# Queries two chunks ahead, weights, gates and o placed behind the turning of a chunk, and z added in the third group of weights

## The chip, the cores and the metric

The kernel is one program on one core of a Trainium2 chip. The metric is the device time of one execution in microseconds (us): the median of three runs before was 2944.49 us (2940.36 to 2946.38). The core has the engines TensorE (PE; its weight loads are listed apart as PEld), VectorE (DVE), ScalarE (ACT) and GpSimd (POOL), and SyncE (SP), which here only issues DMAs. Each engine works through its own instructions in their order and waits on semaphores for the others. A DMA is issued by an engine (here SP and POOL) and moved by 16 DMA engines.

## The reference

With N = 1250 nodes, D = 1024 features, E = 40000 edges, the program computes a graph convolution and then one transformer layer with experts:

```
x = x + gnn(layernorm(x))            # h = x W^T + b, normalised sum over the edges and self loops
z = layernorm(x)
q, k = rope(z Wq[h]), rope(z Wk[h])  # 16 heads of 64
gv = top2of8(sigmoid(z Wsel_v[h]))   # a gate for each of 8 experts, all but two are 0
v = sum_e gv[e] * (z Wv[h, e])
o = softmax(q k^T / 8) v
go = top2of8(sigmoid(z Wsel_o[h]))
src = z + sum_h sum_e go[h, e] * (o Wo[h, e])
src = ln(src, ln1); out = x + ln(src + relu(src W1 + b1) W2 + b2, ln2)
```

All is in float32. The kernel gets this accuracy from matmuls of a rounded part ("hi") and a remainder ("lo") of each operand: a product is three matmuls (`dot`, L152 to L156), and every operand passes through a copy to hi on ScalarE and a subtraction to lo on VectorE.

## The kernel before

Three stages matter here. All of them lie in blocks of `manual_schedule`, in which every engine, and SP's and POOL's queues of DMAs with them, keeps exactly the order in which the Python code creates the instructions. The code is written as generators that are advanced piece by piece, so a place in a generator is a place in every queue.

**`values` (L872) beside `attention` (L711).** `values` makes v for one head after the other: 40 pieces a head, each of six 512-column matmuls. The expert weights of the next head come as four blocks of 512 KB: `load` (SP, into one of the two `w_raw` buffers), then `first_part` (the copy to hi, ScalarE, L138), then `second_part` (the subtraction to lo, VectorE, L144). The lists of pairs say at which of the 40 pieces each happens for each of the four blocks. Because there are two buffers, a load waits until the `second_part` of the block before the last is done.

`attention` works in 80 chunks (16 heads by 5 chunks of 256 queries), in eight pieces a chunk, and one piece of it is advanced after each piece of `values`. It starts at piece 26, so chunk n's piece p (0 to 7) stands behind `values` piece k where (k - 26) mod 8 = p. The pieces of a chunk n, with what they do for the chunks n - 1 and n - 2 that are still on their way:

- 0: `softmax(n, 0)`: scores of 128 queries (PE, L739), their maximum (DVE, L742), the exponential (ACT, L743); then `load_queries(n + 1)` (POOL)
- 1: `product(n - 2, 2)` (PE, L796); `turn_blocks(n - 1)`: two transposes on DVE (L816)
- 2: `product(n - 2, 3)`; `split(n - 1, 0)` and `(n - 1, 1)`: hi on ACT (L773)
- 3: `softmax(n, 1)`; `load_keys` where the next chunk opens a head; `rest(n - 1, 0)` and `(n - 1, 1)`: lo on DVE (L778)
- 4: `product(n - 2, 4)`, which ends with a copy of o on ACT (L803) and one or two DMAs of o to HBM (POOL); `turn(n)`; after the last chunk of a head the sums (SP); `split(n - 1, 2)`
- 5 to 7: the rest of the splits, and `product(n - 1, 0)` and `(n - 1, 1)`

`turn(n)` (L746) moves the exponentials p into the buffer `turned` by 16 DMAs of 80 KB, each of which brings a block of 32 partitions to another 32: eight on SP and eight on POOL. Then the transposes turn the blocks of 32 by 32 inside. `product(n - 1, 0)` writes to the PSUM tile `po`, of which there is one: it has to wait until the copy of o of the chunk before has read it.

**`outputs` (L935).** 16 groups of weights (8 pairs of heads, two halves of the experts), each with five steps of 250 nodes: 80 steps. A step has two tiles of 125 nodes by two halves of 512 columns: four results of 12 matmuls, each of which is added to the accumulator of its tile (`acc`, L1036). A step takes a block of the next group's weights (SP, 512 KB; not in the fifth step), `gb`, the gates of the step after the next (SP, two DMAs, 500 KB), and the attention's o with its sums for that step (SP, four DMAs or more, `load_o`). `gated` multiplies gates and o (DVE, L967 to L969), and `parts_of` makes hi and lo of it (L976, L978). Each step is eight pieces. The accumulators start as z: `acc_load` reads a tile of z from HBM by two DMAs (`move`, L150), and in the first group it stands two tiles ahead of the tile's first addition. The memory of the accumulators is that of zT, which `values` has read to its end by then.

The first sixteen pieces of `outputs` only prepare; they are advanced with the last 16 of `values`. Then the remaining 42 pieces of `attention` alternate with the first 42 of `outputs`: the first group, and a little. From then on `outputs` runs alone.

**`feed_forward` (L1049)**, after the last group. Its tables (`ftab`) are broadcast rows of 512 KB, loaded by SP.

`tc.issue_after(ins)`, which the change uses, adds an order (no semaphore, no wait for an end) between `ins` and those instructions created in its block that run on the engine of `ins`.

Of the kernel before, what the change touches and what calls it, by code (L numbers as in the profile page):

```python
# [2 lines left out]

# [8 lines left out]
F32 = mybir.dt.float32  # L12
# [5 lines left out]
ALU = mybir.AluOpType  # L18
# [54 lines left out]
def gnn_ffn_kernel(  # L73
# [631 lines left out]


    v_of = {}

    def attention(pool):

# [102 lines left out]

        def turn_blocks(n):
            for i in range(2):
                nc.vector.transpose(turned[n][:, i], turned[n][:, i])  # L816

        load_keys(0)
        load_queries(0)
        for n in range(len(chunks) + 2):  # L820
            now, last, before = (0 <= m < len(chunks) for m in (n, n - 1, n - 2))

            if now:
                softmax(n, 0)
            if before:
                rest(n - 2, 4)
            if n + 1 < len(chunks):
                load_queries(n + 1)
            yield
            if before:  # L830
                product(n - 2, 2)
            if last:
                turn_blocks(n - 1)
            yield
            if before:
                product(n - 2, 3)
            if last:
                split(n - 1, 0)
                split(n - 1, 1)
            yield  # L840
            if now:
                softmax(n, 1)
                if n + 1 < len(chunks) and chunks[n + 1][1] == 0:
                    load_keys(chunks[n + 1][0])
            if last:
                rest(n - 1, 0)
                rest(n - 1, 1)
            yield
            if before:
                product(n - 2, 4)  # L850
            if now:
                turn(n)
# [12 lines left out]
            if last:  # L865
                product(n - 1, 1)
                split(n - 1, 4)
                rest(n - 1, 3)
            yield


    def values(att_pool, pool, now):  # L872
# [8 lines left out]
        for h in range(H):  # L881
            raw, new = {}, [None] * 4

            def load(h, k, raw=raw):
                raw[k] = loaded(wv[h, k])

            def first_part(k, raw=raw, new=new):
                new[k] = high(raw[k])
# [3 lines left out]

            if h + 1 < H:

                for at_, k in ((22, 0), (36, 1), (37, 2), (39, 3)):
                    later(piece + at_, first_part, k)
                for at_, k in ((23, 0), (37, 1), (38, 2), (40, 3)):
                    later(piece + at_, second_part, k)
                for at_, k in ((16, 0), (22, 1), (28, 2), (37, 3)):
                    later(piece + at_, load, h + 1, k)  # L900
            v_of[h] = att_pool.tile([P, NT, P], F32R, name="v2", bufs=2)

# [29 lines left out]

    acc = []

    def outputs(acc_pool, pool):  # L935

        last = QW * (NC - 1)

# [43 lines left out]
        blocks = {k: [wo[j, 4 * half_e + i] for i in range(4)] for k, (j, half_e) in enumerate(order)}  # L982
        steps = [(k, c) for k in range(len(order)) for c in range(NQ)]

        def acc_load(t):
            acc.append(acc_pool(t))
            move(acc[t], z_d[t])

        def fetch(m, gates):
            if m < len(steps):  # L990
# [4 lines left out]
                    held[:] = load_o(j, c)  # L995


        w, raw, found, held, parts = [], [], [], [], []
        for begun in range(16):
            if begun < 2:  # L1000
                raw.append(loaded(blocks[0][begun]))
            if begun in (3, 4, 7, 8):
                w.append(rounded(raw.pop(0)))
            if begun in (3, 4):
                raw.append(loaded(blocks[0][begun - 1]))
            if begun == 4:
                fetch(0, True)
                fetch(0, False)
            if begun == 5:
                acc_load(0)  # L1010
            if begun == 9:
                current = gated(found.pop(0), *held)
                fetch(1, True)
                fetch(1, False)
            if begun in (11, 13):
                parts.append(parts_of(current, len(parts)))
            if begun == 14:
                acc_load(1)
            yield
        after = []  # L1020
        for m, (k, c) in enumerate(steps):
            raw = loaded(blocks[k + 1][c]) if c < 4 and k + 1 < len(order) else None
            following = m + 1 < len(steps)
            fetch(m + 2, True)
            for i in range(2):
                t = 2 * c + i
                if k == 0 and t + 2 < NT:
                    acc_load(t + 2)
                for half in range(2):
                    cols = slice(512 * half, 512 * half + 512)  # L1030
                    p = bank([KT, 512])
                    for e in range(4):
                        dot(p, [part[:, e, :] for part in parts[i]], [part[:, cols] for part in w[e]], e == 0, e == 3)
                        if e == 1:
                            yield
                    nc.vector.tensor_tensor(acc[t][:, cols], acc[t][:, cols], p, ALU.add)  # L1036
                    if following and half:
                        parts[i] = parts_of(current, i)
                    elif following and i == 0:
                        current = gated(found.pop(0), *held)  # L1040
                        fetch(m + 2, False)
                    elif raw is not None:
# [62 lines left out]

    f_ctx = ctx.enter_context(ExitStack())
    per_head = 4 * NT
    main, spare = [], []

    def acc_tile(t):  # L1110

# [10 lines left out]
    with tc.tile_pool(name="attp", bufs=1) as apool:  # L1122
        w = [weights(wv[0, k]) for k in range(4)]
        with tc.manual_schedule(engines=all_engines):
            heads = attention(apool)
            with tc.tile_pool(name="vpool", bufs=2) as vpool:
                for k, _ in enumerate(values(apool, vpool, w)):
                    if k >= per_head - lead:
                        next(heads)
                    if k == H * per_head - 4 * NZ - 1:  # L1130
                        z2_ctx.close()
                        ring[:0] = [ctx.enter_context(tc.tile_pool(name="ring2", bufs=3, side="right"))] * 3
                        gop = ctx.enter_context(tc.tile_pool(name="gop", bufs=1, side="right"))
                        main.append(outputs(acc_tile, gop))
                    elif main:
                        next(main[0])
            made = sum(1 for _ in zip(heads, main[0]))
    main = main[0]
    p_ctx.close()
    banks[:] = [5, 2]  # L1140
    psums.append(p_ctx.enter_context(tc.tile_pool(name="psum3", bufs=1, space=PSUM)))
    ftab = f_ctx.enter_context(tc.tile_pool(name="ftab", bufs=1))
    work = f_ctx.enter_context(tc.tile_pool(name="fwork", bufs=2))
    tail = feed_forward(ftab, work)
    with tc.manual_schedule(engines=all_engines):
        for _ in range(4 * (NT * (2 * NP - 1) + 4) - made):
            next(main)
    next(tail)
    for _ in main:
# [77 lines left out]
```

## Time and profile before

| | |
|---|---|
| median of three runs | 2944.49 us (2940.36 to 2946.38) |
| the profiled execution | 2949.87 us, its span 2948.1 us |
| granted clock of TensorE | 0.990 of full speed over the span |
| `values` beside `attention` | about 640 to 1840 us |
| first group of `outputs` beside the last chunks | about 1840 to 1970 us |
| `outputs` alone | about 1970 to 2780 us |
| VectorE's idle time before the transposes (L816) | 135.3 us |

The page of a profile lists for each engine its busy time. A group of instructions is given as line, engine, operation, output<-inputs, shape and count; then busy time, the mean of one in nanoseconds, the idle time of the engine just before them, and what ended most of it. A row of waits reads: who waited <- for whom: us in total, times, longest. A row of windows reads: stretch, its length, then the busy time and the number of instructions of PE, PEld, DVE, ACT and POOL, the granted clock of TensorE, the DMA engines' busy share, and GB/s. A row of the timeline reads: start, length, engine (SPq is SP's queue of DMA issues), line, operation, tiles, shape, count, and in brackets the idle time before it and what ended that. Rows of DMA queues give packets, MB and the share of the 16 engines' time.

### The profile page before, as it was taken

Reading aid. Unit: us, or ns where it says so; the run is one execution under the profiler, and the core shown is the slowest. Engines: PE = TensorE matmul, PEld = TensorE weight load, DVE = VectorE, ACT = ScalarE, POOL = GpSimd, SP = SyncE. Lnnn points to the kernel's source line nnn. Section 1 sums busy time; section 2 is a strip of 40 time slices with the busy share of each in tenths; the row PEclk is TensorE's granted clock in tenths of the full one; section 3 lists DMA queues with packets and bytes.
Section 4 is the critical chain, followed back from the end, with each engine's and each line's share of the span. In section 5 each row is a group of like instructions: output and inputs, shape, how many; then the busy total and the mean of one; then the engine's idle time right before and its main releaser. Section 6 shows DMA issues by size and latency. Waiting matters only on the chain. (4 is left out here: it accounts for less than half of the span.)

```text
span 2948.1 us, 40387 instructions
## 1 busy us (share of the span) xinstructions
PE 2845.5 (97%) x14018; PEld 2346.9 (80%) x14018; DVE 2118.5 (72%) x3588; ACT 996.7 (34%) x1708; POOL 570.3 (19%) x945
## 2 busy tenths in 40 slices
PE   6989999999999999999999999899999999999998
PEld 5777899978888887788888888677777777777787
DVE  7975786558777877878777777866566666666885
ACT  5772333324443433434343434421111111111222
POOL 2000011123333333333333333210000000000113
PEclk9999999999999999999999999999999999999999
DMA  3115466635645555555555555874444444444412
GB/s 118 57 44 159 146 182 177 191 90 137 154 130 147 133 136 123 128 149 138 146 138 139 139 145 126 213 204 126 115 120 122 115 119 122 112 122 117 112 53 88
DMA packets 229319, 385.45 MB, mean 131 GB/s; under 512 B 43369, under 2 KB 176489, under 8 KB 228946
## 3 DMA queue, kind: packets, MB, share of 16 engines
q1 hardware_dynamic: 176898, 273.49, 33.3%
q0 software_dynamic: 51888, 104.18, 14.6%
q10 hardware_dynamic: 320, 5.12, 0.6%
q8 instruction: 111, 1.82, 0.3%
q14 instruction: 102, 0.84, 0.1%
HBM read 220.73 MB, written 62.16 MB: 96 GB/s over the span
## 5 line engine op out<-in xcount | busy, mean ns | idle before, releaser
L155 PE MATMUL mm<-w_lo,zT 128*128 128x512 f32 (+2 forms) x1360 | 528.9, 389 | 3.8 <-DVE w_lo L144 3.3
L154 PE MATMUL mm<-w_hi,zT 128*128 128x512 f32 (+2 forms) x1360 | 529.7, 390 | 0.8 <-ACT w_hi L138 0.8
L156 PE MATMUL mm<-w_hi,zT 128*128 128x512 f32 (+2 forms) x1360 | 528.4, 389 | 0.0
L154 PE MATMUL mm<-w_hi,go_hi 128*125 128x512 f32 x1280 | 507.2, 396 | 3.7 <-ACT go_hi L976 2.8
L155 PE MATMUL mm<-w_lo,go_hi 128*125 128x512 f32 x1280 | 507.4, 396 | 0.0
L156 PE MATMUL mm<-w_hi,go_lo 128*125 128x512 f32 x1280 | 503.8, 395 | 0.0
L773 ACT CAST att_hi<-turned 128x512 fp32r<-128x512 f32 x400 | 239.9, 622 | 460.1 <-DVE turned L816 286.7
L754 POOL DMA_DIRECT2D turned<-p x640 | 343.9, 545 | 78.9 <-ACT p L743 44.5
L1036 DVE TENSOR_TENSOR zT<-zT,mm 125x512 f32<-125x512 f32 x256 | 175.5, 686 | 221.1 <-PE mm L156 216.8
L816 DVE STREAM_TRANSPOSE turned<-turned 128x1280 f32<-128x1280 f32 x160 | 232.4, 1491 | 135.3 <-DMA q<-kq_d 62.4
L976 ACT CAST go_hi<-gb 128x500 fp32r<-128x500 f32 x160 | 98.3, 616 | 660.0 <-PE mm L155 281.8
L742 DVE TENSOR_REDUCE most<-side 128x1 f32<-128x1250 f32 x160 | 231.0, 1444 | 111.7 <-PE side L739 109.1
L743 ACT ACTIVATE p<-side,most 128x1250 f32<-128x1250 f32 x160 | 209.2, 1308 | 290.3 <-DVE most L742 285.7
L156 PEld LDWEIGHTS mm<-w_hi,zT 128*128 128x128 f32 (+1 forms) x1360 | 253.1, 186 | 59.9
L154 PEld LDWEIGHTS mm<-w_hi,go_hi 128*125 128x125 f32 x1280 | 237.9, 186 | 65.2 <-ACT go_hi L976 3.5
L155 PEld LDWEIGHTS mm<-w_lo,zT 128*128 128x128 f32 (+1 forms) x1360 | 253.3, 186 | 43.9 <-DVE w_lo L144 8.6
L156 PEld LDWEIGHTS mm<-w_hi,go_lo 128*125 128x125 f32 x1280 | 237.9, 186 | 61.7 <-DVE go_lo L978 0.5
L155 PEld LDWEIGHTS mm<-w_lo,go_hi 128*125 128x125 f32 x1280 | 237.6, 186 | 58.2
L154 PEld LDWEIGHTS mm<-w_hi,zT 128*128 128x128 f32 (+1 forms) x1360 | 253.7, 187 | 35.6 <-ACT w_hi L138 1.0
L778 DVE TENSOR_TENSOR att_lo<-turned,att_hi 128x512 fp32r<-128x512 f32 x400 | 262.3, 681 | 0.0
L796 PE MATMUL po<-att_hi,v 128*128 128x256 f32 (+1 forms) x800 | 216.1, 291 | 38.1 <-ACT o L803 38.0
L144 DVE TENSOR_TENSOR w_lo<-w_raw,w_hi 128x1024 fp32r<-128x1024 f32 x154 | 189.4, 1231 | 35.7 <-ACT w_hi L138 35.2
(227 smaller groups left out, 4501.9 us busy)
## 6 DMA issues: line engine op xcount, KB each, us to landing
turned<-p SPq DMA_DIRECT2D x640, 80.0 KB
turned<-p POOLq DMA_DIRECT2D x640, 80.0 KB, 3.3
gb<-g_d SPq DMA_DIRECT2D x160, 250.0 KB
w_raw<-in_wv SPq DMA_DIRECT2D x64, 512.0 KB
w_raw<-in_wo SPq DMA_DIRECT2D x64, 512.0 KB
q<-kq_d POOLq DMA_DIRECT2D x80, 256.0 KB, 4.2
oc<-o_d SPq DMA_DIRECT2D x160, 125.0 KB
kq_d<-qk_hi SPq DMA_DIRECT2D x64, 156.2 KB
```

Source lines behind the costliest of these rows:

```text
L144: (lo_engine or nc.vector).tensor_tensor(lo, raw, hi.bitcast(F32), ALU.subtract)
L154: nc.tensor.matmul(p, lhsT=lhs[0], rhs=rhs[0], start=start, stop=False)
L155: nc.tensor.matmul(p, lhsT=lhs[0], rhs=rhs[1], start=False, stop=False)
L156: nc.tensor.matmul(p, lhsT=lhs[1], rhs=rhs[0], start=False, stop=stop)
L742: nc.vector.tensor_reduce(most, side[:, :N], AX.X, ALU.max, negate=True)
L743: nc.scalar.activation(p[:, (2 * n + i) % 3, :N], side[:, :N], AF.Exp, bias=most, accum_out=inverse[h][:, 2 * c + i : 2 * c + i + 1])
L754: queue.dma_start(t[NB * a : NB * (a + 1), :, KA * b : KA * (b + 1)], both[NB * b : NB * (b + 1), :, KA * a : KA * (a + 1)])
L773: nc.scalar.copy(hi, x)
L778: nc.vector.tensor_tensor(lo, x, hi.bitcast(F32), ALU.subtract)
L796: nc.tensor.matmul(po, lhsT=v_of[h][:rows, t, :], rhs=part[:rows, :, NB * b : NB * (b + 1)], start=(first and b == 0 and part is parts[0]) ...
L816: nc.vector.transpose(turned[n][:, i], turned[n][:, i])
L1036: nc.vector.tensor_tensor(acc[t][:, cols], acc[t][:, cols], p, ALU.add)
```

## The change

- `attention`: `load_queries` of the first two chunks at the start; that of chunk n + 2 in piece 3 of chunk n, after `softmax(n, 1)`, instead of that of n + 1 in piece 0.
- `turn_blocks` keeps its last transpose in `landed`. The loads of `values`, and in `outputs` the loads of weights, gates and o, are created in a block of `issue_after(landed[0])` as long as `attention` runs.
- `values`: the next head's blocks 0 and 1 are loaded at pieces 20 and 21 (16 and 22 before), and block 0 is split at 24 and 25 (22 and 23 before).
- `outputs`: the three loads of a step stand together behind the step's first tile (fourth of its eight pieces), in the order weights, gates, o; before, weights and gates stood at its beginning, and o in its second piece. The rounding of the block goes from the sixth piece to the eighth.
- The accumulators are no longer loaded with z. In the first group a result is copied to its accumulator; in the third group each tile of z is loaded into a buffer (two of them, SP) and added one tile later (`add_z`, DVE, 125 x 1024).
- The pool of these buffers takes the memory that the feed-forward's tables get after it, so these pools are opened after the fourth group.

```diff
+    landed = []
...
         def turn_blocks(n):
             for i in range(2):
-                nc.vector.transpose(turned[n][:, i], turned[n][:, i])
+                landed[:] = [nc.vector.transpose(turned[n][:, i], turned[n][:, i]).ins]
 
         load_keys(0)
-        load_queries(0)
+        for n in range(2):
+            load_queries(n)
...
-            if n + 1 < len(chunks):
-                load_queries(n + 1)
...
                 softmax(n, 1)
                 if n + 1 < len(chunks) and chunks[n + 1][1] == 0:
                     load_keys(chunks[n + 1][0])
+                if n + 2 < len(chunks):
+                    load_queries(n + 2)
...
             def load(h, k, raw=raw):
-                raw[k] = loaded(wv[h, k])
+                with tc.issue_after(landed[0]) if landed else nullcontext():
+                    raw[k] = loaded(wv[h, k])
...
-                for at_, k in ((22, 0), (36, 1), (37, 2), (39, 3)):
+                for at_, k in ((24, 0), (36, 1), (37, 2), (39, 3)):
                     later(piece + at_, first_part, k)
-                for at_, k in ((23, 0), (37, 1), (38, 2), (40, 3)):
+                for at_, k in ((25, 0), (37, 1), (38, 2), (40, 3)):
                     later(piece + at_, second_part, k)
-                for at_, k in ((16, 0), (22, 1), (28, 2), (37, 3)):
+                for at_, k in ((20, 0), (21, 1), (28, 2), (37, 3)):
                     later(piece + at_, load, h + 1, k)
...
-        def acc_load(t):
-            acc.append(acc_pool(t))
-            move(acc[t], z_d[t])
+        def add_z(t):
+            nc.vector.tensor_tensor(acc[t], acc[t], zs.pop(0), ALU.add)
...
         for m, (k, c) in enumerate(steps):
-            raw = loaded(blocks[k + 1][c]) if c < 4 and k + 1 < len(order) else None
+            raw = None
             following = m + 1 < len(steps)
-            fetch(m + 2, True)
             for i in range(2):
                 t = 2 * c + i
-                if k == 0 and t + 2 < NT:
-                    acc_load(t + 2)
+                if k == 0:
+                    acc.append(acc_pool(t))
...
-                    nc.vector.tensor_tensor(acc[t][:, cols], acc[t][:, cols], p, ALU.add)
+                    if k == 0:
+                        nc.vector.tensor_copy(acc[t][:, cols], p)
+                    else:
+                        nc.vector.tensor_tensor(acc[t][:, cols], acc[t][:, cols], p, ALU.add)
+                    if k == 2 and half:
+                        if t:
+                            add_z(t - 1)
+                        zs.append(later[0].tile([KT, D], F32, name="z"))
+                        move(zs[-1], z_d[t])
+                    elif k == 3 and half and t == 0:
+                        add_z(NT - 1)
                     if following and half:
                         parts[i] = parts_of(current, i)
                     elif following and i == 0:
                         current = gated(found.pop(0), *held)
-                        fetch(m + 2, False)
-                    elif raw is not None:
+                    if half and i == 0:
+                        with tc.issue_after(landed[0]) if landed else nullcontext():
+                            if c < 4 and k + 1 < len(order):
+                                raw = loaded(blocks[k + 1][c])
+                            fetch(m + 2, True)
+                            fetch(m + 2, False)
+                    elif half and raw is not None:
                         after.append(rounded(raw))
                     yield
...
             made = sum(1 for _ in zip(heads, main[0]))
+            landed.clear()
...
-    ftab = f_ctx.enter_context(tc.tile_pool(name="ftab", bufs=1))
-    work = f_ctx.enter_context(tc.tile_pool(name="fwork", bufs=2))
-    tail = feed_forward(ftab, work)
     with tc.manual_schedule(engines=all_engines):
-        for _ in range(4 * (NT * (2 * NP - 1) + 4) - made):
+        with tc.tile_pool(name="later", bufs=2) as pool:
+            later.append(pool)
+            for _ in range(4 * NT * 4 - made):
+                next(main)
+        ftab = f_ctx.enter_context(tc.tile_pool(name="ftab", bufs=1))
+        work = f_ctx.enter_context(tc.tile_pool(name="fwork", bufs=2))
+        tail = feed_forward(ftab, work)
+        for _ in range(4 * (NT * (2 * NP - 1) + 4) - 4 * NT * 4):
             next(main)
```

The calls of `acc_load` in the sixteen preparing pieces (pieces 5 and 14) go too.

More of the change, by code (lines that the diff above doesn't have):

```diff
@@ L1 @@
-from contextlib import ExitStack
+from contextlib import ExitStack, nullcontext
 from itertools import cycle, islice
@@ L933, in gnn_ffn_kernel, with outputs @@
     acc = []
-    def outputs(acc_pool, pool):
+    def outputs(acc_pool, pool, later):
         last = QW * (NC - 1)
@@ L995, in fetch @@
                     held[:] = load_o(j, c)
-        w, raw, found, held, parts = [], [], [], [], []
+        w, raw, found, held, parts, zs = [], [], [], [], [], []
         for begun in range(16):
@@ L1008, in outputs @@
                 fetch(0, False)
-            if begun == 5:
-                acc_load(0)
             if begun == 9:
@@ L1016, in outputs @@
                 parts.append(parts_of(current, len(parts)))
-            if begun == 14:
-                acc_load(1)
             yield
@@ L1107, in gnn_ffn_kernel @@
     per_head = 4 * NT
-    main, spare = [], []
+    main, spare, later = [], [], []
     def acc_tile(t):
@@ L1133, in gnn_ffn_kernel @@
                         gop = ctx.enter_context(tc.tile_pool(name="gop", bufs=1, side="right"))
-                        main.append(outputs(acc_tile, gop))
+                        main.append(outputs(acc_tile, gop, later))
                     elif main:
```

## The prediction

> **What bounds the kernel now.** Read first the page's busy table, then TensorE's waits, then windows over the stages, then the timelines of the places that wait.
>
> ```profile
> PE 2845.5 (97%) x14018; PEld 2346.9 (80%) x14018; DVE 2118.5 (72%) x3588; ACT 996.7 (34%) x1708; POOL 570.3 (19%) x945
> ```
>
> TensorE is the bound, so only its idle time and its slow time can be won. The waits of TensorE from 640 to 1840 us (`values` beside `attention`) and from 1840 to 1970 us (`outputs` beside the last chunks) have one line that matters, in total, times, longest:
>
> ```profile
> PE po L796 <- ACT o L803: 20.2, 27, 3.5
> ...
> PE po L796 <- ACT o L803: 17.7, 5, 6.1
> ```
>
> The windows of the three stages:
>
> ```profile
> 640.00:1840.00 1200.00, 1175.95 (x5854) 973.04 (x5853) 943.40 (x1264) 487.38 (x791) 433.38 (x775) 1.00 0.54 138
> 1840.00:1970.00 130.00, 111.40 (x526) 91.37 (x525) 98.29 (x130) 47.13 (x77) 31.55 (x57) 0.95 0.81 201
> 1970.00:2780.00 810.00, 809.99 (x3482) 644.06 (x3483) 511.71 (x729) 149.69 (x212) 8.35 (x3) 1.00 0.46 124
> ```
>
> The third stage has nothing to win. The second loses 18.6 us of 130 idle, at DMA share 0.81 and clock 0.95. The chain behind its longest wait (VectorE and ScalarE timeline):
>
> ```profile
> 1928.27 2.91 DVE L816 STREAM_TRANSPOSE turned<-turned 128x1280 f32<-128x1280 f32 x2 [5.41 <-DMA zT<-z_d]
> ...
> 1932.25 1.45 DVE L742 TENSOR_REDUCE most<-side 128x1 f32<-128x1250 f32 x1
> ...
> 1933.73 1.30 ACT L743 ACTIVATE p<-side,most 128x1250 f32<-128x1250 f32 x1 [1.34 <-DVE most L742]
> ...
> 1935.03 1.03 ACT L138 CAST w_hi<-w_raw 128x1024 fp32r<-128x1024 f32 x1
> 1935.96 0.37 ACT L803 COPY o<-po 128x256 f32<-128x256 f32 x1
> ```
>
> VectorE stands still until the turned chunk lands; the maximum, the exponential and the copy of o queue behind it, and TensorE waits for that copy. The landing is late because the second half of the turning DMAs (POOL's) is passed by SP's traffic. The same in the first stage at 1174 us (SP's queue is q1, POOL's q0), where POOL's last three turning DMAs took 5.1 us to land against 3.3 us in the median:
>
> ```profile
> q1 hardware_dynamic: 80, 0.32, 85.7%
> q0 software_dynamic: 18, 0.04, 10.4%
> ```
>
> After a long wait the clock is lost too. Windows around the stalls of 3.5, 1.6 and 6.1 us (the clock is the third number from the end):
>
> ```profile
> 1850.00:1862.00 12.00, 8.51 (x34) 6.79 (x33) 11.06 (x16) 7.03 (x11) 2.36 (x5) 0.86 0.76 205
> ...
> 1911.00:1919.00 8.00, 6.39 (x32) 5.03 (x31) 6.67 (x11) 4.78 (x8) 4.35 (x9) 1.00 0.93 228
> 1926.00:1944.00 18.00, 11.87 (x47) 9.57 (x46) 12.25 (x18) 6.02 (x10) 4.86 (x9) 0.81 0.63 159
> ```
>
> 12 x 0.14 = 1.7 us and 18 x 0.19 = 3.4 us of clock went; after 1.6 us none.
>
> **Base.** The profiled execution took 2949.87 us (span 2948.1 and 1.8 around it), 5.4 us over the median 2944.49. Differences are worked out in it and put on the median. This kernel's runs spread 0.2%, 5.9 us; less can't be told from no change.
>
> **1. The wait that the words promise.** `issue_after(ins)` orders only those instructions of its block that run on the engine of `ins`. `landed[0]` is a VectorE transpose; the blocks hold only SP's DMAs. I take it that no edge arises: 0 us, and SP still issues as soon as its queue and the buffers allow. So places in SP's order count, not phases.
>
> **2. `acc` no longer loaded in the first group** (20 DMAs, 5.1 MB on SP). Before the turning at 1858.91, SP issued these two from 1857.52: it starts 1.4 us earlier, and the 5.0 us stall behind it shrinks by that. At 1920 us they stand behind w and gates, between which POOL's last turning DMAs took 7.1 us to land; bounds 0 (w and gates alone suffice) and 3.8 (landing as in the median); I take 1.8, as SP's first megabyte stays. -3.2 us.
>
> **3. `rounded(raw)` from the third to the fourth quarter's end.** Its 1.03 us cast (0.93 until the copy starts) leaves the place between the exponential and the copy of o in the stalls at 1895, 1913 and 1935: -2.8 us. It stands later behind `go_hi`, with the next group's use a whole step away; VectorE's 1.23 us goes along. Bounds 0 and -2.8.
>
> **4. Clock.** With 2 and 3 the 6.1 us stall becomes 3.4, and I take half of its 3.4 us of lost clock as won: -1.7 (bounds 0 and -6.8, all three).
>
> **5. Weights of `values`.** Loads 0 and 1 go from pieces 16 and 22 to 20 and 21. SP's order then has both, 1 MB, right behind the turning of piece 14: nothing lies between, and their buffers were freed at 38 and 40. Before, one 0.5 MB load stood there and the other behind the next turning. It matters where POOL ends after SP: every third chunk has two stores of o before POOL's turning (at 1166.50), and in 5 of 14 heads that chunk is this one. Their stalls were up to 1.5 us. The first load already takes the landing of POOL's last two or three from 3.3 to between 4.3 and 5.1 us in four of the five; the second is as long, but only what is left of the tail pays. 1.2 us each, +6; bounds 0 (the tail is through) and 1.8 x 5 = +9. A stall of 1.9 us (1216 us) did lose clock 13 x 0.13 = 1.7 us, one of 1.5 us didn't; I take one such, +2 (bounds 0 and +8.5). Load 2 now waits for `rounded` at piece 25, so behind the next turning stands nothing at first: the 3.5 us stall at 1109 to 1115 us, where POOL was 4 us late and met both loads, should lose about 2 (bounds 0 and -5.2 with its clock). The cast at piece 24 instead of 22 lies in ScalarE's idle (34% busy), the subtraction before VectorE's wait for scores (109 us in all): 0; uncovered 15 x 1.23 us in time that is no stall now.
>
> **6. Queries two ahead.** POOL's 0.74 us issue and 256 KB go from behind the turning to before the store of o, where POOL waits for ScalarE anyway (459 us in 51 waits). POOL's own turning stood before them in the ring, so only SP's last turning DMAs can gain. VectorE's waits before the transposes are put down to q for 62.4 us in 37, 1.7 each, but a landing close by is as likely the cause; a tenth of a microsecond for each of 27 stalls, -3 (bounds 0 and -6). They wait for TensorE's scores, over well before the exponential.
>
> **7. z in the third group.** Ten additions like `w_lo` (1.25 us), 12.5 us on VectorE, in a stage where it is 63% busy: two in an 11.1 us step make it 86%. Loads 1 MB more in a step, 124 to some 215 GB/s, the rate that 1840 to 1970 us shows as possible. Five PSUM banks of 12 matmuls (0.23 us each) give TensorE some 10 us of cover; 0, at worst +2. Copies instead of additions in group one: 0. Tables of the feed-forward move from 1967 us to later, read at 2750: 0.
>
> Sum: -3.2 - 2.8 - 1.7 + 6 + 2 - 2 - 3 = -4.7, taken as -5: 2939.5 us.
>
> **A rule against the row.** The Trainium skill, *DMA: Bandwidth & Descriptors*, Queues, rings and completion order, says that each DMA engine takes turns between its queues packet by packet. By it POOL's tail keeps half of each engine however much SP queues, the second load costs nothing, and the sum would be -13. The row (85.7 against 10.4%) speaks for unequal shares, and I go by it. The skill's *TensorE: Matmul & The Clock Gate*, part 1, puts the halving after an idle window of some 3.4 us; by it the +2 would be 0, but the stall of 1.9 us disagrees.
>
> **Rivals.**
> *The tail escapes* (faster): with a quarter of the stage's traffic gone the 6.1 us stall falls to 1 us and keeps its clock (-8.5), the others win 1.4 and 2 x 0.93 (-3.3), the second load finds POOL's tail landed (0), and 5's -2 and 6's -3 stay: -16.8, about 2927.5 us. For it: TensorE never waits from 1970 us on, at DMA share 0.46. Against: w and gates still stand behind SP's turning.
> *The second load starves POOL* (slower): each of five chunks grows by 1.8 us and four lose the clock, +9 + 6.8, queries gain 0, and of the rest only 4.2 (points 2 and 3 without the landing) and 2 are won: about +10, 2954 us. It passes +6 from 2.4 us a chunk on, clock included ((6 + 6.2) / 5). For it: 85.7%; against: by the packet records only 35 to 110 KB of the tail are left by then.
> *SP does wait for VectorE*: then loads no longer meet the turning (-4.5 for the late chunks, -2 and -3 as in 5 and 6, -11 in the outputs), but eight issues of some 0.65 us fall between the transposes and the next turning, which starts 1.5 us late five times (+7.5): -13, 2931.5 us. Against it: point 1.
>
> **How the numbers follow.** Forecast 0.42 (own range 2932 to 2949: of it 0.30 within 0.2%, 0.10 faster, 0.02 slower); tail escapes 0.28 (0.26 faster); starved 0.22 (0.21 slower); SP waits 0.08 (0.04 faster, 0.03 same). Faster 0.40, same 0.36, slower 0.24. The range leaves about a tenth on each side: 2926 to 2953.
>
> **What would show it.** SP: two weight loads directly behind every fifth turning, without a gap, and none until about 6 us after the next one's end; an SP that idles until the transposes end would overturn point 1. Waits of po for o: below 12 us in all from 1840 to 1970, with no `w_hi` between exponential and o; and in 3 of the 5 late chunks above 2 us. No idle TensorE in the third group. I am wrong if the late chunks don't move, or if stalls come up where none was.

## The result and the profile after

The changed kernel takes 2924.18 us in the median of six runs (2918.87 to 2931.36), the kernel before 2944.23 us in six runs beside them (2940.36 to 2950.07). The ratio is 0.9932, its 95% interval 0.9913 to 0.9951: 20 us faster, with 14 and 26 us as the interval's ends. In a second comparison on another chip (e9 below) the ratio was 0.9915 (0.990 to 0.993), 25 us. The forecast was 5 us faster, in a range whose lower end, 2926, lies 1.8 us above the measured time. The sign was the likelier one of the stated chances; the size was a quarter of the truth, and the largest part came from a term that the forecast had put at 3 us.

The two profiled executions lie further apart than the medians: 2949.87 and 2919.96 us, 29.9 apart. So the parts found in this pair add up to more than the change is worth. Cut at the ends of attention's exponentials (the second half of each chunk), which mark the same point of the work in every trace:

| stretch | before, us | after, us | difference |
|---|---|---|---|
| up to the end of chunk 0's exponential | 623.2 | 620.1 | -3.1 |
| chunks 0 to 73 (`values` beside `attention`) | 1196.8 | 1180.2 | -16.6 |
| chunks 73 to 79 (`outputs` beside `attention`) | 115.0 | 107.6 | -7.4 |
| after it | 1013.0 | 1010.2 | -2.8 |

The first row holds work that the change leaves alone but for one early load of queries; in the other profiles shown below it lies between 622 and 630 us, so its 3 us are no effect that could be told from variation. The large term is the second row, where the forecast had expected a loss.

The busy table after, in whole, with each engine's share of the span:

```profile
PE 2831.9 (97%) x14018; PEld 2342.7 (80%) x14018; DVE 2137.0 (73%) x3598; ACT 996.6 (34%) x1708; POOL 569.2 (20%) x945
```

TensorE has the same instructions and was at 97% before as well: the busy table shows the result only as 13.6 us less busy time, and the trace doesn't say by which instructions. The windows of the three stages after (columns: window and its length, busy us of TensorE, its weight loads, VectorE, ScalarE and GpSimd, then clock, DMA share, GB/s):

```profile
640.00:1840.00 1200.00, 1181.25 (x5916) 984.03 (x5916) 959.17 (x1277) 497.06 (x803) 433.70 (x777) 1.00 0.55 140
1840.00:1970.00 130.00, 121.56 (x573) 98.30 (x572) 101.29 (x136) 42.32 (x71) 25.09 (x46) 0.99 0.65 162
1970.00:2780.00 810.00, 804.28 (x3463) 639.49 (x3462) 539.03 (x755) 151.26 (x220) 16.86 (x6) 1.00 0.48 126
```

In the second window, where the forecast had looked for its gain, the DMA share fell from 0.81 to 0.65, the clock rose from 0.95 to 0.99, and 18.6 us without work became 8.4. In the first, the same 1200 us now hold 5916 matmuls instead of 5854, 1.1% more, though TensorE's idle time shrank by 5 us only. The windows are fixed in time, and the work after runs up to 27 us earlier against them, so for amounts the table of chunks above is the one to use.

TensorE's waits in the first window, then in the second (in total, times, longest):

```profile
PE po L797 <- ACT o L804: 10.1, 7, 2.3
...
PE po L797 <- ACT o L804: 6.0, 3, 3.3
```

The waits for the copy of o went from 20.2 to 10.1 us and from 17.7 to 6.0, the longest from 6.1 to 3.3. Divided at the end of chunk 73's exponential instead of at 1840 us, it is 20.2 to 7.8 and 17.7 to 8.3.

One row changed more than any wait of TensorE. The transposes of the turned chunk in the page's groups before (busy, mean ns, then VectorE's idle time ahead of them and its main releaser):

```profile
L816 DVE STREAM_TRANSPOSE turned<-turned 128x1280 f32<-128x1280 f32 x160 | 232.4, 1491 | 135.3 <-DMA q<-kq_d 62.4
```

and after:

```profile
L817 DVE STREAM_TRANSPOSE turned<-turned 128x1280 f32<-128x1280 f32 x160 | 232.3, 1490 | 80.2 <-DMA turned<-p 45.8
```

VectorE waits 55 us less for the turned chunks, and q is gone as a releaser. The experiments show that the larger part of the time came from here, though it is less than half of these 55 us.

### The profile page after: what moved, and what is told of

It is laid out like the page before. It is cut to its first block, busy times and chain, and to the rows that moved or that the text cites. A ratio compares the mean times of both kernels' runs of the same rounds, so it can differ in the third digit from the quotient of the medians.

```text
span 2918.2 us, 40412 instructions
## 1 busy us (share of the span) xinstructions
PE 2831.9 (97%) x14018; PEld 2342.7 (80%) x14018; DVE 2137.0 (73%) x3598; ACT 996.6 (34%) x1708; POOL 569.2 (20%) x945
## 5 line engine op out<-in xcount | busy, mean ns | idle before, releaser
L1037 DVE TENSOR_TENSOR zT<-zT,mm 125x512 f32<-125x512 f32 x240 | 164.5, 686 | 201.0 <-PE mm L156 194.4
```

## The experiments

What each run should decide: which part of the change carries the gain, and whether a turned chunk that lands earlier is worth its whole time in every chunk (the closed chain, "R" in the texts below) or only where TensorE would have stood still, as point 6 of the prediction had it. Ratios are each against the kernel before on the same chip, turned into microseconds with that chip's median of before (2951.36, 2951.69 and 2949.19 for the three sets).

**e1: the queries' move alone, on the kernel before.**

```diff
-        load_queries(0)
+        for n in range(2):
+            load_queries(n)
...
-            if n + 1 < len(chunks):
-                load_queries(n + 1)
...
+                if n + 2 < len(chunks):
+                    load_queries(n + 2)
```

> The kernel before with the queries' move alone (all else as before). Theory Q (the first stage's gain is the queries': their 256 KB no longer follow the turning, so that the last turning DMAs land sooner): -8 to -14 us against before, waits of po for o in the first stage from 20 us to about 12, the landing of SP's last turning DMA some 0.3 us sooner. Theory L (the gain is that of the moved weight loads): -3 us or less, as the prediction had it.

Measured: 0.9923 (0.9908 to 0.9939), 23 us faster; repeated on another chip as e10: 0.9939 (0.9925 to 0.9954), 18 us. The part that was forecast at 3 us carries nearly the whole result, more than either theory of the text above expected. Chunks 0 to 73 take 1174.3 us in its profile, 22.5 less than before.

**e2: the moved loads and splits of `values` alone.**

```diff
-                for at_, k in ((22, 0), (36, 1), (37, 2), (39, 3)):
+                for at_, k in ((24, 0), (36, 1), (37, 2), (39, 3)):
...
-                for at_, k in ((23, 0), (37, 1), (38, 2), (40, 3)):
+                for at_, k in ((25, 0), (37, 1), (38, 2), (40, 3)):
...
-                for at_, k in ((16, 0), (22, 1), (28, 2), (37, 3)):
+                for at_, k in ((20, 0), (21, 1), (28, 2), (37, 3)):
```

> The kernel before with the moved loads and splits of the weights in values alone. Theory L: -8 to -14 us. Theory Q: within 3 us of before; the five late chunks may lose 1 to 2 us in all. The prediction's own terms (+6 +2 -2): +6 us.

Measured: 1.0006 (0.9991 to 1.0020), +2 us and not told from nothing. In the packet records the two effects of point 5 are both there: from the exponential's end to the landing, the chunk whose turning is followed by both loads went from 9.68 to 9.94 us, the next one from 9.18 to 8.93. They cancel, and so do the stalls of TensorE behind them: the five late chunks of the forecast stall for 6.5 us in all instead of 3.3, and the one long stall of before, at 1112 to 1116 us, went from 3.5 to 0.6.

**e3: the rest alone (outputs, z, the blocks of `issue_after`)**, that is, the changed kernel with the queries and the loads of `values` as before. Against the changed kernel:

```diff
-        for n in range(2):
-            load_queries(n)
+        load_queries(0)
...
+            if n + 1 < len(chunks):
+                load_queries(n + 1)
...
-                if n + 2 < len(chunks):
-                    load_queries(n + 2)
...
-                for at_, k in ((20, 0), (21, 1), (28, 2), (37, 3)):
+                for at_, k in ((16, 0), (22, 1), (28, 2), (37, 3)):
```

The splits go back to pieces 22 and 23 likewise.

> The kernel before with the part in outputs alone (z added in the third group, the loads of a step together, rounding in the last piece). Both theories: -6 to -10 us, all of it between 1840 and 1970 us, as in the prediction (-7.7). If the changed kernel's stalls there went by the queries' move, -3 us or less.

Measured: 0.9978 (0.9966 to 0.9990), 6.5 us faster. The forecast for these points was 7.7.

**e4: the changed kernel with the queries as before.** Against the changed kernel:

```diff
-        for n in range(2):
-            load_queries(n)
+        load_queries(0)
...
+            if n + 1 < len(chunks):
+                load_queries(n + 1)
...
-                if n + 2 < len(chunks):
-                    load_queries(n + 2)
```

> The changed kernel with the queries' loads as before. Theory Q: 8 to 14 us slower than the changed kernel, so 6 to 12 us faster than before. Theory L: within 3 us of the changed kernel, 17 to 20 us faster than before. If the parts add up, this is the sum of the second and third kernel.

Measured: 0.9991 (0.9977 to 1.0004), 3 us faster and not told from nothing (the interval's ends are 7 us faster and 1 slower), less than the 6 to 12 expected. Without the queries' move the change would have stayed near the forecast.

So it is the queries: alone they win 18 to 23 us, and without them 3 are left. An earlier issue could help in two ways: the queries arrive earlier, or their 256 KB no longer travel while the turned chunk does. And it has to be told how that can be worth 20 us, when all of TensorE's waits for o in the two stages came to 38. The next set asks both.

**e5: e1 and 256 KB behind the turning again.** The queries stay two chunks ahead; where the old load stood, GpSimd issues a copy of the same size from one place in HBM to another. Nothing reads its result.

```diff
+            nc.gpsimd.dma_start(again_d[n % 2][:], kq_d[h][:, 1:, c0 : c0 + QW])
...
-                load_queries(n + 1)
+                again(n + 1)
```

> The queries' move alone, and in the old place (on POOL, behind the turning) a copy of the same 256 KB to a scratch in HBM that nobody reads. If the move wins because these bytes no longer run beside the last turning DMAs, the gain goes again: within 5 us of before, SP's last landing back at 2.75 us. If it wins because the queries come earlier (some wait for them that the profile put down to others), it stays at -19 to -23 us.

Measured: 1.0011 (0.9994 to 1.0029), +3 us: with the bytes back, the gain is gone, though the queries are as early as in e1. So their earlier arrival isn't what carries it. The transposes' row in its page:

```profile
L822 DVE STREAM_TRANSPOSE turned<-turned 128x1280 f32<-128x1280 f32 x160 | 232.4, 1491 | 140.4 <-DMA again_d<-kq_d 51.2
```

The idle time is back at 140 us, and put down to a copy that VectorE doesn't wait for at all: the row names the transfer that was under way, the true cause is the turning that it slowed. By the chunks' mean period (table below) the first stage lost 15 us of e1's 22. The 6 us that stay go with a landing that is still 0.07 us sooner than before. What else lies between e1 and e5 isn't the bytes', for e6 below has it too. The six chunks beside `outputs` take 115.8 us in both profiles, and what follows them takes 4.8 us longer in e5: there GpSimd starts the turning of the last chunk 5.4 us after its exponential's end, in e1 2.5. GpSimd's timeline, e1 and then e5, and TensorE's wait that comes of it in e5:

```profile
1918.34 4.28 POOL L754 DMA_DIRECT2D turned<-p  x8 [0.32 <-DVE some L760]
...
1936.92 4.26 POOL L760 DMA_DIRECT2D turned<-p  x8 [3.25 <-DMA turned<-p]
...
1953.48 0.58 PE L802 MATMUL po<-att_hi,v 128*128 128x256 f32 x1 [5.29 <-ACT o L809]
```

TensorE then has a mean clock of 0.76 from 1948 to 1962 us. Why GpSimd waits there is open. A copy within HBM also writes there, which a load of queries doesn't; whether that matters was not tried.

**e6: the same with two rows of the copy, 2 KB instead of 256 KB**, so that the issue stays and the bytes go. Again nothing reads them.

```diff
+            nc.gpsimd.dma_start(again_d[n % 2][:1], kq_d[h][:1, 1:, c0 : c0 + QW])
```

> The same with two rows of 1 KB instead of 256 KB: the issue on POOL and its semaphore stay, the bytes don't. Bytes theory: -18 to -23 us against before, as the move alone. If the issue (0.74 us on POOL) or the order of POOL's semaphores was the cost: within 5 us of before.

Measured: 0.9962 (0.9949 to 0.9974), 11 us faster, where 18 to 23 were expected if it is the bytes. In the first stage it is e1 again: waits of 8.4 us for o, and the same period. In the window behind it, it isn't:

```profile
PE po L802 <- ACT o L809: 8.4, 9, 2.4
...
PE po L802 <- ACT o L809: 18.8, 6, 4.5
```

(first the window 640 to 1840, then 1840 to 1970; e1 has 8.9 and 12.8.) So the first stage's gain is the bytes' and not the issue's. The 4.5 us are the stall that e5 has too: here as well GpSimd starts the last chunk's turning 5.4 us after its exponential, and the mean clock is 0.76 over the 14 us around the stall (1936 to 1950 us). The six chunks before that take 115.7 us, as in e1, and what follows them 7.1 us longer. That is most of the 7 to 12 us by which e6 is behind e1; another 3.5 us of its profile lie ahead of the end of chunk 0's exponential, where the first row of the table above varies as much from profile to profile.

**e7: a pause of half a microsecond on VectorE behind the transposes, on the kernel before.** Two maxima over a constant matrix in each chunk, whose result is unused.

```diff
+            for _ in range(2):
+                nc.vector.tensor_reduce(pause, ident, AX.X, ALU.max)
```

> The kernel before with two reductions of a 128 x 128 constant (some 0.2 us each, results unused) on VectorE directly behind the transposes of each chunk. Theory R (a chunk's period is a closed chain: turning lands, transposes, maximum, exponential, next turning; so every tenth of it counts in each of some 75 chunks): +0.4 x 75 = +25 to +33 us, the period from 16.4 to 16.8 us. Theory S (TensorE is the bound, and only the some 27 stalls of the first stage and 5 of the second lengthen): +8 to +14 us.

Measured: 1.0143 (1.0118 to 1.0168), 42 us slower. All reductions, by the view of their line (least, median and most ns):

```profile
L820 DVE TENSOR_REDUCE pause<-ident x160: 241/266/290, 639.8 to 1993.3; 128x1 f32<-128x128 f32 x160
```

160 x 0.266 = 42.6 us. The pieces came out longer than the 0.2 us assumed in the expectation, and with their true length the closed chain's reckoning meets the time: what is put between the landing and the exponential comes out at the end of the stage, in each of its 73 chunks. The period grew by 0.55 us (the table below), and chunks 0 to 73 take 40.5 us longer than before, against 73 x 0.53 = 39. The six chunks beside `outputs` took most of the pause up (115.8 us, 115.0 before), so it is by some chance that the whole meets 160 pieces this closely. Had it only lengthened the stalls that were there, 32 waits for o in the two stages, it would have been 32 x 0.53 = 17 us. Instead new stalls arose, as the waits of the first window show (in total, times, longest) against before's 20.2 us in 27:

```profile
PE po L798 <- ACT o L805: 47.7, 44, 4.9
```

The same pause at a place of VectorE that is not between a landing and an exponential was not tried.

**e8: the changed kernel with a true wait.** The loads of weights and the gates wait for the last transpose by a semaphore; this is the third rival of the prediction, made real.

```diff
+    def waits(dma):
+        if landed:
+            tc.add_manual_dep(dma.ins, landed[0].name,
+                              mybir.DependencyInfo(mybir.DependencyClass.Sync, mybir.DependencyReason.DATA),
+                              reason="after the transposes")
...
-        nc.sync.dma_start(raw, block)
+        waits(nc.sync.dma_start(raw, block))
```

The loads of the gates are wrapped likewise, and the blocks of `issue_after` are taken out.

> The changed kernel with the wait that its words tell of: the loads of weights, gates and o on SP wait by a semaphore for the chunk's last transpose. Theory R: the landing of the turnings in front of weights falls from 9.6 to 8.6 us (one chunk in five), which is worth 0.2 us a chunk where TensorE leaves room: 0 to -8 us against the changed kernel in the first stage; in the second the issues of the loads stand between the transposes and the next turning, +0 to +8. In all -12 to -28 us against before. If the loads' place doesn't matter at all: as the changed kernel, -20.

Measured: 0.9895 (0.9870 to 0.9920), 31 us faster. That suggested that the wait which the words promise would be worth another 10 us if it existed. The last set put that to the test, with all candidates on one chip.

**e9: the changed kernel; e10: e1; e11: the changed kernel with the loads of `values` as before; e12: e8.** e11 against the changed kernel:

```diff
-                for at_, k in ((24, 0), (36, 1), (37, 2), (39, 3)):
+                for at_, k in ((22, 0), (36, 1), (37, 2), (39, 3)):
...
-                for at_, k in ((25, 0), (37, 1), (38, 2), (40, 3)):
+                for at_, k in ((23, 0), (37, 1), (38, 2), (40, 3)):
...
-                for at_, k in ((20, 0), (21, 1), (28, 2), (37, 3)):
+                for at_, k in ((16, 0), (22, 1), (28, 2), (37, 3)):
```

> The changed kernel on the same chip as the next three, so that the parts can be set against the whole. Theory R (each chunk's closed chain sets the first stage) leaves TensorE's own work as the floor at some 16.1 us a chunk; the parts then don't add up: -18 to -24 us against before.

> The queries' move alone once more. If it carries nearly the whole change: within 4 us of the changed kernel. If the parts add up as they did apart (-22 for the queries, +2 for the loads, -6.5 for the outputs): 4 to 5 us slower than the changed kernel.

> The changed kernel with the weights' loads of values as before. If the moved loads cost (a megabyte behind every fifth turning, four of five late chunks still stall): 1 to 5 us faster than the changed kernel; if not, the same within 1 us. By sums of the parts: -28 us against before.

> The changed kernel with the loads of weights, gates and o waiting for the transposes, beside the changed kernel on one chip. Its landing behind weights was 8.7 instead of 9.6 us and the second stage's stalls 5.5 us: 3 to 10 us faster than the changed kernel, and so the fastest of all; if the difference between chips made its -1.05%, the same as the changed kernel.

| run | ratio | 95% | us against before |
|---|---|---|---|
| e9, changed kernel | 0.9915 | 0.9900 to 0.9930 | -25 |
| e10, queries alone | 0.9939 | 0.9925 to 0.9954 | -18 |
| e11, queries and outputs | 0.9899 | 0.9882 to 0.9917 | -30 |
| e12, with a true wait | 0.9915 | 0.9897 to 0.9934 | -25 |

e8's advantage isn't there beside the changed kernel itself: e12 and e9 agree, and e8's ratio had been compared with a ratio from another chip. In e12's records the wait helps the chunk that both loads met (landing after 8.72 us against 9.43 in e9) and sends the loads into the next chunk's turning (9.97 against 8.65), so that the mean landing is no earlier (9.31 against 9.21). e11 is the best of all by its point, 5 us ahead of the changed kernel, but the intervals of the two overlap; the moved loads came out as a loss of 2 to 5 us in all three comparisons that isolate them (e2; e4 against e3; e9 against e11), and in none of them beyond the interval.

## Why: a chain that closes on itself

One chunk of the kernel before, in the timeline of VectorE, ScalarE and GpSimd (start, duration, instruction, and in brackets the idle time before it):

```profile
1148.50 1.31 ACT L743 ACTIVATE p<-side,most 128x1250 f32<-128x1250 f32 x1
...
1151.36 4.29 POOL L754 DMA_DIRECT2D turned<-p  x8 [0.32 <-DVE ve L919]
...
1155.63 0.74 POOL L730 DMA_DIRECT2D q<-kq_d  x1
...
1160.27 2.90 DVE L816 STREAM_TRANSPOSE turned<-turned 128x1280 f32<-128x1280 f32 x2 [2.19 <-DMA q<-kq_d]
1163.09 1.42 DVE L742 TENSOR_REDUCE most<-side 128x1 f32<-128x1250 f32 x1
1164.55 1.31 ACT L743 ACTIVATE p<-side,most 128x1250 f32<-128x1250 f32 x1
```

The exponential ends at 1149.8; its chunk is turned by DMAs; VectorE stands idle for 2.19 us until the turned chunk has landed, transposes it, and directly behind the transposes come the maximum and the exponential of the next chunk, whose end at 1165.9 starts the next turning. That is a closed ring: exponential, turning, landing, transposes, maximum, exponential. In this chunk no step of it waits for TensorE. 2.9 + 1.4 + 1.5 = 5.8 us of it are arithmetic, the rest is transfer. Means over the chunks 2 to 72, in us, from the packet records and the instruction times:

| kernel | SP's half landed | GpSimd's half landed | later of both | landing to transposes | period |
|---|---|---|---|---|---|
| before | 8.94 | 9.04 | 9.54 | 1.08 | 16.39 |
| e1 (queries alone) | 8.79 | 8.90 | 9.21 | 1.03 | 16.10 |
| after | 8.78 | 8.93 | 9.24 | 1.03 | 16.18 |
| e5 (bytes behind) | 9.06 | 8.95 | 9.47 | 1.07 | 16.31 |
| e6 (issue behind) | 8.80 | 8.90 | 9.21 | 1.07 | 16.11 |
| e7 (pause) | 9.13 | 8.99 | 9.64 | 1.13 | 16.94 |

The first three columns are counted from the exponential's end; the chunk has landed when both halves have. In the kernel before, the queries' 256 KB are issued by GpSimd right behind its half of the turning and travel together with the end of both halves. Moved away, they let each half land some 0.15 us sooner in the mean and the later of the two 0.33. e5 puts the bytes back, and SP's half is as late as it was; e6 puts back the issue alone, and it isn't. Between these two only the bytes differ: 0.26 us of SP's landing, 0.05 of GpSimd's, 0.26 of the later of both, and 0.20 of the period.

The profiles of the other runs fall into the same two groups, on whatever chip: with the queries in the old place (e2, e3, e4) the period is 16.36 to 16.46 us, with them moved (e8 to e12) 16.11 to 16.14.

The period follows: 0.29 us x 73 chunks = 21 us for e1, 0.21 x 73 = 15 for the profiled execution of the change. Not all that the transposes' start gains (0.38 us in e1, 0.35 after, the two columns together) is kept: a quarter to two fifths is given back between it and the exponential's end. There the maximum waits for TensorE's scores more often: behind 30 of the 72 transposes it starts over 0.15 us late after the change, behind 8 before. From 640 to 1840 us VectorE's waits for scores went from 100 to 119 us.

How much more is to be had by this way? An estimate: TensorE is busy for about 15.9 us a chunk in the stage (1181.25 of 1200 us, times a period of 16.18), so the period could fall by another 0.2 to 0.3 us, some 20 us in all, before TensorE itself is the ring. No kernel here came below 16.10.

Of e1's 22.5 us in the stage, 13 appear as less waiting of TensorE above 0.15 us (24.3 to 11.2 us between the marks) and some 3 as clock that wasn't lost. The rest I can't place in single waits; matmuls overlap, and their ends are modelled in the profile.

## The prediction, point by point

**1, no wait arises: right.** A kernel with the `issue_after` blocks taken out has the same instructions in the same order on every engine. SP's queue in the profile after has the loads directly behind the turning, as foretold; the load after them came 3 us behind the end of the next turning, not 6 (1180.10 us):

```profile
1136.29 21.15 SPq L755 DMA_DIRECT2D turned<-p  x16
1157.48 1.36 SPq L127 DMA_DIRECT2D w_raw<-in_wv  x2
```

**2 to 4, outputs: right in size.** Forecast -7.7, measured alone -6.5 (-10 to -3). In e3's profile the waits for o behind chunk 73's exponential fell from 17.7 to 11.0 us, where points 2 and 3 had forecast 6; the clock that point 4 counted on is not won there (0.96 over 1820 to 1975 us, as before). The mechanism of point 3 is seen in ScalarE's timeline after: the copy of o follows the exponential at once, and the cast comes a microsecond later.

```profile
1906.63 1.30 ACT L744 ACTIVATE p<-side,most 128x1250 f32<-128x1250 f32 x1 [1.34 <-DVE most L743]
...
1907.92 0.36 ACT L804 COPY o<-po 128x256 f32<-128x256 f32 x1
1909.21 1.06 ACT L138 CAST w_hi<-w_raw 128x1024 fp32r<-128x1024 f32 x1
```

"Below 12 us in all from 1840 to 1970" came out as 6.0, or 8.3 from chunk 73's exponential on.

**5, loads of `values`: sign and rough size right, within what can be told.** Forecast +6 (late chunks), +2 (clock), -2 (the next turning), +6 in sum; measured +2 to +5. The five late chunks stall for 0.4, 1.98, 2.3, 0 and 1.2 us after, so one is above 2 us and one just at it, not three, and the last stands where none was before. Together it is 5.9 us, against 3.3 in the same five before; the 4.5 of the prediction's third rival counts two chunks that are not among them. In the three comparisons that isolate the loads their stalls grew by 3 (e2), 6 (e4 against e3) and 2 us (e9 against e11), where 6 was forecast, and the stall behind the next turning shrank by 3 in e2, where 2 was. One of them did lose clock, as foretold (window, then busy us as above, clock third from the end):

```profile
1165.00:1178.00 13.00, 10.66 (x46) 8.56 (x45) 10.72 (x16) 5.50 (x9) 6.06 (x11) 0.87 0.62 158
```

13 x 0.13 = 1.7 us, behind a stall of 2.3 us.

**6, queries: this is the step that failed.** "A tenth of a microsecond for each of 27 stalls, -3 (bounds 0 and -6)": measured -18 and -23. The mechanism was half right: "only SP's last turning DMAs can gain" is seen in the table, but GpSimd's half gains as much. Both factors of the product were wrong. The landing gained 0.33 us, not 0.1; and it counts in each of some 73 chunks, not in 27 stalls. 0.33 x 73 = 24 us, of which 21 reached the period. The first factor was a guess without a row behind it. The second came from a premise set at the beginning, "TensorE is the bound, so only its idle time and its slow time can be won", which holds only if TensorE sets the period. It doesn't in this stage: the ring does, at 16.39 us, and TensorE's work, about 15.9 us, fits into it so closely that it looks like the bound at 97%. What should have told it was already on the page of before, in the view of the transposes' line from 640 to 1840 us: VectorE's idle time before them, by releaser, in us and times,

```profile
  DMA q<-kq_d: 62.4, 37
  DMA turned<-p: 39.7, 23
  DMA r_d<-rows: 9.4, 6
  DMA w_raw<-in_wv: 8.0, 3
```

that is, a wait in 69 chunks of 73. An instruction that waits in nearly every turn of a loop, and whose successors run straight into the next turn's start, is likely to be on the loop's ring; e7 is the test of it. The prediction read the 62.4 us, called a nearby landing "as likely the cause", which was right (e6's 2 KB are still named for 37.9 of 102.0 us), and then priced it by TensorE's stalls.

**7, z in the third group: right at 0.** From 1985 to 2060 us, where the additions run, TensorE has no idle time:

```profile
1985.00:2060.00 75.00, 75.00 (x325) 59.69 (x324) 54.71 (x75) 11.85 (x18) 0.00 (x0) 1.00 0.75 193
```

VectorE is busy for 73% of it, the DMA engines for 75%.

**The rivals.** "The tail escapes" named 2927.5 us, nearest to the result, but for other reasons: its gain lay in the outputs (-11.8) and not in the queries (-3). "The second load starves POOL" is spoken against by e2, which is +2 with 6 as the interval's end. "SP does wait" is excluded by point 1; made real in e8 and e12 it was worth 31 and 25 us, and beside the change itself on the same chip (e12, e9) no more than that. No rival had the ring, so the range reached 2926 only by the outputs, and the parts as measured, -18 to -23, -6.5 and +2 to +5, add up to -20 to -28 around the -20 and -25 that the whole showed. The sign of the forecast came from the outputs, -7.7 against +6 for the loads; what these parts gave without the queries (e4) is not told from nothing, so that it came true is in part luck.

**The rules weighed there.** The Trainium skill, *DMA: Bandwidth & Descriptors*, Queues, rings and completion order, has each DMA engine alternate between its queues packet by packet. For the second load the runs lie between that rule's 0 and the forecast's +6. For the queries the rule points the right way: by it a transfer on GpSimd's queue takes turns with the end of SP's turning, and e5 against e6 shows a delay of SP's half, 0.26 us for 256 KB (landed after 9.06 against 8.80). No run here shows the alternation itself. The clock's rule, an idle window of some 3.4 us in *TensorE: Matmul & The Clock Gate*, part 1, again differs from a row here: clock was lost behind 2.3 us.

## What to carry to other kernels

Where a loop runs over several engines and DMAs, follow it from one turn's event to the same event of the next turn, and add up the steps: if they make the whole period, a microsecond on any of them counts once per turn, whatever the busy shares say. An engine that is busy for 97% can still be a follower: here a pause of 0.53 us elsewhere cost its whole length in every turn. And a transfer can cost the loop time though nobody in the ring waits for it, if it travels while a landing is awaited. The row of the waiting instruction may name it as the releaser, but that proves nothing: e5's 256 KB and e6's 2 KB are both named, and only the first cost anything in the first stage. Here it paid to move the issue to before the turning.

## What the runs showed of the hardware

- 256 KB on GpSimd's queue, issued within a microsecond behind its own turning DMAs, delay the landing of SP's 640 KB by 0.26 us in the mean and that of GpSimd's own, issued before it, by 0.05 (e5 against e6). The landing of the whole chunk, the later of both, moved by more than either half's mean did when the queries left (0.33 against 0.15 and 0.14): what counts in a loop is the mean of the later one.
- TensorE's clock was cut behind stalls of 1.9 us (before) and 2.3 us (after), but not behind two others of 2.0 and 2.3 us in the profile after (at 928 and 1836 us). The length of the stall alone doesn't decide it.
- A maximum over 128 x 128 elements takes 0.27 us on VectorE.
